# A slot of an attention pipeline put in another order: scores before values, left-over transpositions later

## The chip, the core and the metric

The kernel runs on one core of a Trainium2 chip. The core has a matrix engine (PE; its weight loads are shown apart as PEld), a vector engine (DVE), a scalar engine (ACT), a general engine (POOL) and a queue that issues the DMAs (SP). Each engine takes its instructions strictly in the order in which the kernel emits them, and they wait for each other through semaphores. The metric is the time of one launch on the device in microseconds (us).

## The reference

`x` is [8, 256, 512], eight batch entries. Four layers follow each other, each added to `x`:

```
x = x + L0(x, cond)        # masked self-attention, 8 heads, queries = keys = values
x = x + L1(x, cond)        # modulated RMS-norm, qkv, normalised q and k, attention of 16 heads, o + o @ W_out
x = x + L2(cond, cond, x)  # 256 Runge-Kutta steps, one after the other
x = x + L3(cond, x)        # a GRU cell, 256 steps
```

What matters of the two attentions:

```
L0:  q = x^T Wq^T;  scores = q q^T / sqrt(32), masked;  ctx = softmax(scores) q;  out = ctx Wo^T
L1:  xn = rmsnorm(x) * g * (1 + scale) + shift;  q, k, v = xn W_qkv;  q, k = rmsnorm per head
     o = softmax(q k^T / sqrt(32)) v;  result = o + o W_out
```

## The kernel before

`attention` computes L0 and L1 for all eight entries; `scans` then computes L2 and L3 step by step and is not touched by the change. `scans` starts at about 929 us of the profiled span.

**Slots.** `attention` is a loop over slots `g` from -5 to 79 (line 463), eight slots per batch entry (`U = 8`). L0 of entry `b` has eight units, (half `e` of the heads) x (key block `kc`); unit n is scored in slot 8b+n-4 (`scores0`), weighted in slot 8b+n+1 (`weights0`) and multiplied with the values in slot 8b+n+2 (`values0`). The L1 work of an earlier entry is spread over the same slots. Once all stages run, a round of eight slots repeats; the table names a slot by `g` modulo 8, and lists what it has besides one unit each of scores, values, weights and maxima.

| g mod 8 | further work in the kernel before |
| --- | --- |
| 1 | `weigh0`; transposition of k, part 1; qkv product of q, part 0; first half of x2 (`modulated_out`) |
| 2 | turn of that half (`modulated_turn`); transposition of q, part 0; `masked_out`; qkv of q, part 1; second half of x2 |
| 3 | turn of the second half; transposition of q, part 1; `project` of the entry after next, `normalize`, `maxima1` (needs the transposed q), `rows0` |
| 4 | `project_out`, `modulate`, `project`, `rows1`, `maxima1`, `weights1` |
| 5, 6 | `project_out` and `weigh0` (5 only), qkv of v, `rows1`, `maxima1`, `values1`, `weights1` |
| 7 | qkv of k, part 0; `rows1`, `values1`, `weights1`, `rows0` |
| 0 | transposition of k, part 0; qkv of k, part 1; `values1` |

**The order inside a slot** is written out by hand (lines 464 to 517), and so is the order on every engine's queue. Left-over work of the slot before comes first (`leave`), then values, scores and weights of L0, then the transposition of q or k that the slot before left (`qkv_out`), and then everything else.

**Units of work.** `scores0` (L192): four products of a 32-row block (L198) into four PSUM banks, evicted by four ACT copies (L203) into a tile `sc`. `maxima0` (L206): one DVE maximum over `sc` (L208). `rows0`: transposes the maxima of four units (L216), copies the row out (L218), sends it to DRAM (L221) and back as the broadcast tile `bc` (L222). `weights0` (L224): DVE subtracts `bc` (L226), ACT takes the exponential (L227). `values0` (L229): two sets of four products (L238) into two banks of their own. `weigh0`: two DVE reciprocals and products (L255, L256), then two POOL operations (L257, L258), which make `ctxT`. `masked_out` (L260): output product of L0 (L265), added by DVE (L268). `qkv` (L300): a product (L305); for q and k two ACT readings (L318, L320), a DVE sum (L326), three POOL operations (L328 to L330) in `qkv_norm`, and in a later slot four transpositions (L340) and an ACT copy (L344) in `qkv_out`. `normalize`: ACT squares (L277), two POOL operations, ACT scaling (L282). `modulated_out` (L401): a product (L405) and a DVE addition (L410). `modulated_turn` (L418): four transpositions (L421), an ACT copy (L426) and a DMA (L428).

**Buffers.** All products but those of L238 take their PSUM banks from one pool of six, tag `s` (L57, L60), handed out in turn, so that an allocation waits for the readers of the sixth one before it. The two banks of L238 are freed by `weigh0`. In SBUF there are six `sc` tiles, four `x` tiles (loaded by L74, read last by L410) and two `bc` tiles.

Of the kernel before, what the change touches and what calls it, by code (L numbers as in the profile page):

```python
# [8 lines left out]
F32 = mybir.dt.float32  # L9
# [5 lines left out]
P = 128  # L15
B, T, D = 8, 256, 512
# [8 lines left out]
def attention(ctx, tc, cst, x, cond, wqT, woT, w_emb, b_emb, g_norm, w_qkv, g_q, g_k, w_out, follow):  # L25
# [21 lines left out]
    U = 8  # L47
# [3 lines left out]
    two = ctx.enter_context(tc.tile_pool(name="a_two", bufs=2))  # L51
# [18 lines left out]
    xs, mks = {}, {}  # L70

    def load(b):
        xs[b] = two.tile([P, 2, D], F32, tag="x", name=f"x_{b}", bufs=4)
        nc.sync.dma_start(xs[b], x[b].rearrange("(k p) t -> p k t", p=P))  # L74
        mks[b] = fone.tile([P, D], F32, tag="mk", name=f"mk_{b}", bufs=2)
        nc.sync.dma_start(mks[b], cond[b].partition_broadcast(P))
# [115 lines left out]
    def scores0(b, e, kc):  # L192

        qm = qms[b]
        ss = [bank([P, D], f"s0_{b}_{e}_{kc}_{h}") for h in range(4)]
        for h in range(4):
            r = 32 * h
            nc.tensor.matmul(  # L198
                ss[h], lhsT=qm[r : r + 32, e, kc * P : (kc + 1) * P], rhs=qm[r : r + 32, e, :], start=True, stop=True
            )  # L200
        sc = ftwo.tile([P, 4, D], F32, tag="sc", name=f"sc_{b}_{e}_{kc}", bufs=6)
        for h in range(4):
            nc.scalar.copy(sc[:, h, :], ss[h])  # L203
        scs[b, e, kc] = sc
# [7 lines left out]
    def rows0(b, e):  # L212

        pt = bank([P, NJ, P], f"pm0_{b}_{e}")
        for qc in range(NJ):
            nc.tensor.transpose(pt[:, qc, :], mxp0[e][:, qc, :], ident)  # L216
        mrow = ftwo.tile([P, D], F32, tag="mrow", name=f"mrow0_{b}_{e}", bufs=1)
        nc.scalar.copy(mrow, pt.rearrange("p q n -> p (q n)"))  # L218
        bc = bcs[b, e] = ftwo.tile([P, 4, D], F32, tag="bc", name=f"bc_{b}_{e}")
        row = dram.tile([4, D], F32, tag="row", name=f"row_{b}_{e}", bufs=2)  # L220
        nc.sync.dma_start(row, mrow.rearrange("(h i) n -> h i n", i=32)[:, 0, :])  # L221
        nc.sync.dma_start(bc, row.rearrange("h n -> (h n)").partition_broadcast(P).rearrange("p (h n) -> p h n", h=4))  # L222
# [6 lines left out]
    def values0(b, e, kc):  # L229
        if kc == 0:  # L230
            if e == 0:
                ctxTs[b] = fone.tile([P, 2, D], F32, tag="ctxT", name=f"ctxT_{b}")
            pc0s[b, e] = [ps_c.tile([P, D], F32, tag=f"c{i}", name=f"pc0_{b}_{e}_{i}") for i in range(2)]
        sc = scs.pop((b, e, kc))
        for half in range(2):
            for h in range(4):
                o = e * P + h * DH
                nc.tensor.matmul(  # L238
                    pc0s[b, e][half][32 * h : 32 * h + 32, :],
                    lhsT=qtoks[b][:, kc, o : o + DH] if half == 0 else ones[:, 0:DH],  # L240
                    rhs=sc[:, h, :],
                    start=(kc == 0),
                    stop=(kc == NJ - 1),
                )
# [55 lines left out]
    def qkv(b, part, m):  # L300

        n = f"{b}_{m}_{part}"
        ps = bank([P, D], f"psqkv_{n}")
        for c in range(NJ):
            nc.tensor.matmul(  # L305
                ps,
                lhsT=xnTs[b][:, c, m * P : (m + 1) * P],
                rhs=wqkv_sb[:, c, part * D : (part + 1) * D],
                start=(c == 0),
                stop=(c == NJ - 1),  # L310
            )
        if part == 2:
            if m == 0:
                vts[b] = two.tile([P, 2, D], F32, tag="vt", name=f"vt_{b}", bufs=2)
            nc.scalar.copy(vts[b][:, m, :], ps)
            return None
        sq = line(f"sq_{n}")
        nc.scalar.activation(sq, ps, AF.Square)  # L318
        qr = line(f"qr_{n}")
        nc.scalar.copy(qr, ps)  # L320
        return sq, qr
# [15 lines left out]
    def qkv_out(b, part, m, qr):  # L337
        pt = bank([P, NJ, P], f"ptqk_{b}_{m}_{part}")
        for c in range(NJ):
            nc.tensor.transpose(pt[:, c, :], qr[:, c * P : (c + 1) * P], ident)  # L340
        ts, tag, g = ((qTs, "qT", gqs), (kTs, "kT", gk_sb))[part]
        if m == 0:
            ts[b] = two.tile([P, NJ, 256], F32, tag=tag, name=f"{tag}_{b}", bufs=1)
        nc.scalar.activation(ts[b][:, :, m * P : (m + 1) * P], pt, AF.Copy, scale=g)  # L344
# [56 lines left out]
    def modulated_out(b, m):  # L401
        n = f"{b}_{m}"
        ps = bank([P, D], f"psx2_{n}")
        for c in range(NJ):
            nc.tensor.matmul(  # L405
                ps, lhsT=oTs[b][:, c, m * P : (m + 1) * P], rhs=wout_sb[:, c, :], start=(c == 0), stop=(c == NJ - 1)
            )
        x2 = line(f"x2_{n}")

        nc.vector.tensor_tensor(  # L410
            x2.rearrange("p (m j i) -> p j m i", j=NJ, m=NJ),
            ps.rearrange("p (j m i) -> p j m i", j=NJ, m=NJ),
            xs[b][:, m, :].rearrange("p (j m i) -> p j m i", j=NJ, m=NJ),
            ALU.add,
        )
        return x2
# [18 lines left out]
    for b in range(B):  # L435
        per = 2 if b >= B - 2 else 1
        norms.append(U * b + U + (2 if b == B - 1 else 3))
        start = norms[b] + (2 if b != B - 2 else 3)
        for i, part in enumerate(PARTS):
            parts.setdefault(start + i // per, []).append((b, *part))  # L440
        HEADS.append(start + len(PARTS) // per)
        OUT.append(HEADS[b] + 6)

    def at(g, rel, n=1):

        b, r = divmod(g - rel, U)
        return (b, r) if 0 <= b < B and r < n else None
# [10 lines left out]
    def leave(kind):  # L458
        for key in [k for k in left if k[0] == kind]:
            yield *key[1:], left.pop(key)  # L460

    with tc.manual_schedule():
        for g in range(-5, OUT[-1] + 3):
            for a in leave("qt"):
                project_out(*a)
            if g == OUT[-1] + 2:
                cst["soon"]()
            for a in leave("x2"):
                modulated_turn(*a)
            if g - 1 in norms:  # L470
                modulate(norms.index(g - 1))
            if a := at(g, 2, U):
                values0(a[0], a[1] // 4, a[1] % 4)
            if a := at(g, -4, U):
                scores0(a[0], a[1] // 4, a[1] % 4)
            if a := at(g, 1, U):
                weights0(a[0], a[1] // 4, a[1] % 4)
            if (a := at(g, 2, U)) and a[1] % 4 == 3:
                weigh0(a[0], a[1] // 4)
            for a in leave("qkv"):  # L480
                qkv_out(*a)

            if a := at(g, -5, 2):
                left["qt", a[0], a[1]] = project(*a)
            if a := at(g, U + 2):
                masked_out(a[0])
            if g == 4:
                modulation()
            if g in norms:
                normalize(norms.index(g))  # L490
            made = [(part, qkv(*part)) for part in parts.get(g, ())]
            for b in range(B):
                if g - OUT[b] in (0, 1):
                    left["x2", b, g - OUT[b]] = modulated_out(b, g - OUT[b])

            for part, lines in made:
                if lines:
                    qkv_norm(*part, *lines)
                    left["qkv", *part] = lines[1]
            if a := heads(g, 1):  # L500
                rows1(*a)
            a, a1 = at(g, -4, U), heads(g, 0)
            last = a and a[1] % 4 == 3
            if last:
                maxima0(a[0], a[1] // 4, 3)
            if a1:
                maxima1(*a1)
            if a2 := heads(g, 2):
                values1(*a2)
            if a2 := heads(g, 1):  # L510
                weights1(*a2)
            if a and not last:
                maxima0(a[0], a[1] // 4, a[1] % 4)
            if last:
                rows0(a[0], a[1] // 4)
            if (a2 := at(g, -7)) and a2[0] > 1:
                load(a2[0])
            if g == U * B + 2:
                first.close()
                follow()  # L520
                for (b, m), d in x2d.items():
                    nc.sync.dma_start(
                        cst["x2T"][:, :, b, m * P : (m + 1) * P], d.rearrange("p (j n) -> p j n", j=NJ)
                    )
# [486 lines left out]
```

## Time and profile before

| | |
| --- | --- |
| device time, median of three runs | 3015.35 us (3013.42 to 3015.56) |
| the profiled execution: its time / its span | 3006.1 us / 3004.3 us |
| mean granted clock of PE in it | 0.973 |
| `attention` / `scans` in the span | 0 to about 929 us / 929 to 3004 us |
| PE, busy share of the span | 90% |
| DVE / ACT / POOL, busy share | 71% / 57% / 35% |
| L305 (qkv products), x384 | 177.0 us busy, 607 ns each |
| L226 (subtraction of the maxima), x64 | 150.1 us busy, 2345 ns each |
| L208 (maxima), x64 | 145.7 us busy, 2279 ns each |
| L203 (score evictions), x256 | 131.1 us busy, 604 ns each |
| L227 (exponentials), x64 | 129.5 us busy, 2024 ns each |

A row of groups gives an instruction's line, its count, its busy time and the idle time of its engine just before it, with what ended it. The profiled execution is 9.25 us shorter than the median of the three timed runs; a sum is made against its own 3004.3 us of span.

### The profile page before, as it was taken

How to read it: one execution, taken by the hardware profiler on the slowest of the kernel's cores; microseconds unless marked ns; L12 is line 12 of the kernel's file. 1: busy time of each engine (PE TensorE's matmuls, PEld its weight loads, DVE VectorE, ACT ScalarE, POOL GpSimd, SP SyncE). 2: the span in 40 equal slices, each digit the busy share in tenths (PEclk: the TensorE clock that was granted, in tenths of full speed). 3: DMA queues.
4: the chain of work that ended last, by engine and by line, in shares of the span. 5: the costliest groups of instructions: out<-in, count | busy, mean ns of one | idle time of the engine just before them, and what ended most of it. 6: DMA issues, size and time to landing. Idle time of an engine off the chain costs nothing.

```text
span 3004.3 us, 159873 instructions
## 1 busy us (share of the span) xinstructions
PE 2713.9 (90%) x67258; PEld 1922.1 (64%) x67258; DVE 2129.0 (71%) x8948; ACT 1715.9 (57%) x8427; POOL 1047.1 (35%) x2945
## 2 busy tenths in 40 slices
PE   6679889888998999999999999999999999999997
PEld 2224334433455777777777777777777777777775
DVE  4657667766535777777777777777777777777774
ACT  4456555655335666666666666666666666666652
POOL 0132222222322444444434444444344444443442
PEclk7789999999999999999999999999999999999999
DMA  3010010101050000000000000000000000000000
GB/s 141 25 39 29 32 46 15 47 32 36 22 120 3 5 6 7 6 7 6 6 7 6 6 7 6 7 6 6 7 6 6 7 6 7 7 6 7 6 6 7
DMA packets 27560, 57.60 MB, mean 19 GB/s; under 512 B 2816, under 2 KB 17164, under 8 KB 24788
## 3 DMA queue, kind: packets, MB, share of 16 engines
q1 hardware_dynamic: 26836, 47.36, 5.1%
q8 instruction: 526, 8.62, 1.2%
q14 instruction: 198, 1.62, 0.2%
HBM read 40.15 MB, written 7.21 MB: 16 GB/s over the span
## 4 chain that ended last, share of the span: by engine, by line
PE 55%; DVE 27%; ACT 8%; issue 4%; POOL 4%; ACTq 0%; DMA 0%; POOLq 0%; SPq 0%; DVEq 0%
PE pg L742 19%; PE ic L707 17%; DVE icT L899 5%; DVE qn L900 5%; PE psqkv L305 4%; ACT tT L607 4%; PE pc L238 3%; DVE hqs L860 3%; DVE own L757 3%; DVE sqmm L856 2%; DVE v L759 2%; POOL r L329 2%; PE s L198 2%; PE pc L154 2%; DVE hz L787 2%
## 5 line engine op out<-in xcount | busy, mean ns | idle before, releaser
L707 PE MATMUL ic<-cT_sb,tT 128*8 128x128 f32 x32736 | 1087.5, 273 | 82.4 <-ACT tT L607 44.3
L707 PEld LDWEIGHTS ic<-cT_sb,tT 128*8 128x8 f32 x32736 | 759.1, 89 | 343.1 <-ACT tT L607 272.2
L742 PE MATMUL pg<-whh_sb,hz 128*32 128x128 f32 x24576 | 818.9, 274 | 49.5 <-DVE hz L787 16.2
L607 ACT ACTIVATE tT<-qn 128x16 f32<-128x16 f32 x2046 | 439.9, 216 | 642.4 <-DVE qn L900 563.9
L742 PEld LDWEIGHTS pg<-whh_sb,hz 128*32 128x32 f32 x24576 | 667.8, 110 | 124.0 <-DVE hz L787 123.6
L899 DVE STREAM_TRANSPOSE icT<-ic 128x64 f32<-128x64 f32 x2048 | 503.4, 246 | 68.3 <-PE ic L707 63.4
L900 DVE SCALAR_TENSOR_TENSOR qn<-icT,hqs 128x16 f32<-128x16 f32 x2048 | 350.4, 171 | 70.0
L702 POOL TENSOR_TENSOR W<-W,cx 128x128 f32<-128x128 f32 x765 | 297.3, 389 | 256.4 <-ACT cx L688 256.3
L695 POOL TENSOR_TENSOR W<-cx,us 128x128 f32<-128x128 f32 x255 | 116.9, 458 | 446.5 <-ACT cx L688 446.5
L856 DVE SCALAR_TENSOR_TENSOR sqmm<-sqmm,qn 128x32 f32<-128x32 f32 x768 | 153.5, 200 | 152.4 <-ACT sqmm L845 123.2
L860 DVE TENSOR_TENSOR hqs<-W,sqmm 128x32 f32<-128x32 f32 x1020 | 200.2, 196 | 46.3 <-DVE sqmm L856 1.4
L203 ACT COPY sc<-s 128x512 f32<-128x512 f32 x256 | 131.1, 604 | 139.4 <-PE s L198 139.4
L721 PE MATMUL gi<-wih_sb,x3T 128*32 128x384 f32 (+2 forms) x3072 | 202.4, 379 | 0.5 <-POOL x3T L912 0.5
L688 ACT ACTIVATE cx<-qn 128x32 f32<-128x32 f32 x1280 | 200.8, 213 | 0.1
L305 PE MATMUL psqkv<-wqkv_sb,xnT 128*128 128x512 f32 x384 | 177.0, 607 | 0.0
L688 ACT ACTIVATE cx<-p 128x32 f32<-128x32 f32 x1020 | 149.8, 217 | 32.8 <-DVE p L855 2.0
L208 DVE TENSOR_REDUCE mxp<-sc 128x4 f32<-128x2048 f32 x64 | 145.7, 2279 | 28.1 <-ACT sc L203 28.1
L226 DVE TENSOR_TENSOR sc<-sc,bc 128x2048 f32<-128x2048 f32 x64 | 150.1, 2345 | 4.3 <-DMA bc<-row 4.3
L757 DVE STREAM_TRANSPOSE own<-pg 128x128 f32<-128x128 f32 x256 | 84.9, 332 | 91.8 <-PE pg L742 91.6
L688 ACT ACTIVATE cx<-q 128x32 f32<-128x32 f32 x1020 | 145.6, 213 | 0.0
L227 ACT ACTIVATE sc<-sc,negT 128x2048 f32<-128x2048 f32 x64 | 129.5, 2024 | 22.6 <-DVE sc L226 15.1
L845 ACT ACTIVATE sqmm<-qn 128x32 f32<-128x32 f32 x768 | 140.5, 183 | 0.6
(149 smaller groups left out, 3338.6 us busy)
## 6 DMA issues: line engine op xcount, KB each, us to landing
bc<-row SPq DMA_DIRECT2D x16, 1024.0 KB
x<-in_x SPq DMA_DIRECT2D x8, 512.0 KB
out<-o SPq DMA_DIRECT2D x256, 16.0 KB
wqkv_sb<-in_L_cond_W_qkv SPq DMA_DIRECT2D x1, 3072.0 KB
wih_sb<-in_L_cond_W_ih SPq DMA_DIRECT2D x4, 768.0 KB
whh_sb<-in_L_cond_W_hh SPq DMA_DIRECT2D x4, 768.0 KB
x2d<-x2o SPq DMA_DIRECT2D x11, 256.0 KB
x2T<-x2d SPq DMA_DIRECT2D x11, 256.0 KB
```

The source lines that it names most:

```text
L305: nc.tensor.matmul(ps, lhsT=xnTs[b][:, c, m * P : (m + 1) * P], rhs=wqkv_sb[:, c, part * D : (part + 1) * D], start=(c == 0), stop=(c == N ...
L607: nc.scalar.activation(tT, src[:, half * HM : (half + 1) * HM, :], AF.Tanh)
L688: nc.scalar.activation(c[:, i], x, AF.Copy, scale=f)
L702: nc.gpsimd.tensor_tensor(W[:, i + 1 : 5], W[:, i + 1 : 5], c, ALU.add)
L707: nc.tensor.matmul(ps[32 * j : 32 * j + B, :], lhsT=tT[k // HM][:, k % HM, :], rhs=cT_sb[:, k, j * P : (j + 1) * P], start=(k == 0), stop= ...
L721: nc.tensor.matmul(gi_ps[rows(j), g0:g1, :], lhsT=x3T[c][:, k, :], rhs=wih_sb[:, k, g0:g1, j * P : (j + 1) * P], start=(k == 0), stop=(k = ...
L742: nc.tensor.matmul(pg_ps[rows(j), :], lhsT=hzs[tau % 3][:, k, 32 * g : 32 * g + 32], rhs=whh_sb[:, k, g, j * P : (j + 1) * P], start=((k, ...
L757: nc.vector.transpose(pgt.rearrange("p m n -> p (m n)"), pg_ps)
L856: stt(mm, sq, LIN[s], qs, ALU.subtract, ALU.mult)
L860: nc.vector.tensor_sub(hq, W[:, s], mm)
L899: nc.vector.transpose(icT.rearrange("p m n -> p (m n)"), ic[:, half * 64 : half * 64 + 64])
L900: stt(qn[:, m2, :], icT[:, :, 0:B], IC[s], hq[:, m2, :], ALU.mult, ALU.add)
```

## The change

Five edits. (1) In a slot the scores of L0 come first, then the values, and only then the left-over work of the slot before. (2) `qkv_out`, the transposition of the q or k that the slot before left, moves from behind the weights to behind this slot's own qkv product (and so behind `project`, `masked_out` and `normalize`). (3) The second half of x2 is made two slots after the first instead of one, except for the last two entries; its turn follows one slot later. (4) Seven `sc` tiles instead of six, because a slot's scores are now written before its values free the oldest tile; five `x` tiles instead of four, because an entry's `x` is read one slot longer. (5) One `bc` tile instead of two. The last slot is 79 in both, and the computation is the same.

```diff
-        xs[b] = two.tile([P, 2, D], F32, tag="x", name=f"x_{b}", bufs=4)
+        xs[b] = two.tile([P, 2, D], F32, tag="x", name=f"x_{b}", bufs=5)
...
-        sc = ftwo.tile([P, 4, D], F32, tag="sc", name=f"sc_{b}_{e}_{kc}", bufs=6)
+        sc = ftwo.tile([P, 4, D], F32, tag="sc", name=f"sc_{b}_{e}_{kc}", bufs=7)
...
-        bc = bcs[b, e] = ftwo.tile([P, 4, D], F32, tag="bc", name=f"bc_{b}_{e}")
+        bc = bcs[b, e] = ftwo.tile([P, 4, D], F32, tag="bc", name=f"bc_{b}_{e}", bufs=1)
...
-        OUT.append(HEADS[b] + 6)
+        OUT.append((HEADS[b] + 6, HEADS[b] + (8 if per == 1 else 7)))
...
-        for g in range(-5, OUT[-1] + 3):
+        for g in range(-5, OUT[-1][1] + 2):
+
+            if a := at(g, -4, U):
+                scores0(a[0], a[1] // 4, a[1] % 4)
+            if a := at(g, 2, U):
+                values0(a[0], a[1] // 4, a[1] % 4)
             for a in leave("qt"):
                 project_out(*a)
-            if g == OUT[-1] + 2:
+            if g == OUT[-1][1] + 1:
                 cst["soon"]()
             for a in leave("x2"):
                 modulated_turn(*a)
             if g - 1 in norms:
                 modulate(norms.index(g - 1))
-            if a := at(g, 2, U):
-                values0(a[0], a[1] // 4, a[1] % 4)
-            if a := at(g, -4, U):
-                scores0(a[0], a[1] // 4, a[1] % 4)
             if a := at(g, 1, U):
                 weights0(a[0], a[1] // 4, a[1] % 4)
...
-            for a in leave("qkv"):
-                qkv_out(*a)
...
             made = [(part, qkv(*part)) for part in parts.get(g, ())]
+            for a in leave("qkv"):
+                qkv_out(*a)
             for b in range(B):
-                if g - OUT[b] in (0, 1):
-                    left["x2", b, g - OUT[b]] = modulated_out(b, g - OUT[b])
+                if g in OUT[b]:
+                    m = OUT[b].index(g)
+                    left["x2", b, m] = modulated_out(b, m)
```

## The prediction

> **What bounds it now.** I read the page first, then the time by windows, then PE, ACT and DVE in order of time.
>
> ```profile
> PEclk7789999999999999999999999999999999999999
> PE 55%; DVE 27%; ACT 8%; issue 4%; POOL 4%; ACTq 0%; DMA 0%; POOLq 0%; SPq 0%; DVEq 0%
> L340 PE MATMUL ptqk<-ident,qr 128*128 128x128 f32 x128 | 23.3, 309 | 52.1 <-POOL qr L330 52.1
> L238 PE MATMUL pc<-sc,qtok 128*32 128x512 f32 x512 | 79.4, 697 | 32.1 <-ACT sc L227 32.0
> 243.40:343.86 100.46, 88.70 (x652) 40.78 (x656) 69.07 (x59) 57.24 (x95) 25.38 (x22) 0.98 0.10 35
> 343.86:442.64 98.78, 87.03 (x653) 40.21 (x656) 69.01 (x59) 57.24 (x95) 25.36 (x22) 1.00 0.10 36
> 442.64:541.40 98.76, 87.00 (x652) 40.19 (x656) 68.99 (x59) 57.23 (x95) 25.38 (x22) 1.00 0.10 36
> 541.40:642.89 101.49, 90.21 (x653) 41.55 (x656) 69.00 (x59) 57.23 (x95) 25.38 (x22) 0.97 0.09 35
> 642.89:742.00 99.11, 88.83 (x631) 40.21 (x631) 65.52 (x54) 54.23 (x88) 24.45 (x21) 0.94 0.08 28
> ```
>
> The scans (929 to 3004 us, lines 607 to 900 of the chain) are untouched. Only the first 929 us can change, in three stages: a ramp (slots up to 19, to 243 us), five rounds of eight slots (the windows; columns: length, busy PE, PEld, DVE, ACT, POOL, clock, DMA), and a tail (742 to 929). In a round PE is busy 87.0 of 98.8 us and idle 11.8; no other engine passes 69. So a round ends with PE, and only its idle time can go. In the ramp nothing is full:
>
> ```profile
> 113.48 2.06 PE L198 MATMUL s<-qm 32*128 32x512 f32 x8
> 119.62 1.93 PE L238 MATMUL pc<-sc,qtok 128*32 128x512 f32 x8 [4.08 <-ACT sc L227]
> 115.62 2.05 ACT L203 COPY sc<-s 128x512 f32<-128x512 f32 x4 [5.02 <-PE s L198]
> 117.53 2.03 ACT L227 ACTIVATE sc<-sc,negT 128x2048 f32<-128x2048 f32 x1
> ```
>
> This is a ring. The values wait for the exponential, which stands on ACT's queue behind the evictions of the same slot's scores, and those scores stand on PE's queue behind the values. Values 3.6, scores 2.1, evictions 1.9 and exponential 2.1 follow one another: 9.7 us a slot (values start at 109.91, 119.62, 129.35).
>
> **Edit 1 in the ramp.** With scores first, the evictions run beside the values and the ring is cut. What is late next is DVE: per slot L226 2.20 and L208 2.19 (start to start), every fourth slot `weigh0` 4.25; and `bc`, which arrives some 7.5 us after the last maximum of its four (transposition and row copy 1.2, row DMA 1.75, issue to first use 4.7: 33.57 to 38.28) while DVE has 5 us of other work, so 2 to 2.5 idle per four slots. That is (4 x 4.4 + 4.25 + 2.3)/4 = 6.0 a slot. PE needs 2.9 (5.7 at half clock), ACT 3.9. I walked DVE, ACT and PE through the slots in their new order with these durations, starting at the first `bc`, which DMA brings at 38.28 as before:
> - slots 2 to 4 (42.7 to 80.3): the modulation's 11.3 us of PE stays, the serial parts around it go: 7 saved.
> - slots 5 to 10 (57.6 us): 43, so 14 saved.
> - slots 11 to 16 (57.7): normalisation, then qkv products; DVE-bound, 50, so 8 saved.
> - slots 17 to 19 (47.7): here edit 2 acts. PE waits for POOL 4.09 + 3.78 + 3.78 and then runs slowly (L305 5.54 for 3.60, L265 5.79 for 3.70, L176 3.62 for 1.98: 5.7 more), 17.3 together; less the new waits below and less that DVE's `weigh0` now sets slot 18: 11 saved.
>
> Together 40. Bounds: 25, if only the ring of slots 5 to 10 and half of the POOL waits go; 50, if DVE never waits for `bc`.
>
> **The rounds.** PE's waits in one round (1.34 in slot 4 besides):
>
> ```profile
> 599.76 0.66 PE L340 MATMUL ptqk<-ident,qr 128*128 128x128 f32 x4 [1.58 <-POOL qr L330]
> 608.16 0.63 PE L421 MATMUL ptx<-ident,x 128*128 128x128 f32 x4 [0.88 <-DVE x L410]
> 613.96 1.11 PE L340 MATMUL ptqk<-ident,qr 128*128 128x128 f32 x4 [2.25 <-POOL qr L330]
> 627.34 0.63 PE L421 MATMUL ptx<-ident,x 128*128 128x128 f32 x4 [0.88 <-DVE x L410]
> 633.14 0.66 PE L340 MATMUL ptqk<-ident,qr 128*128 128x128 f32 x4 [2.24 <-POOL qr L330]
> 639.65 0.33 PE L216 MATMUL pm<-ident,mxp 128*128 128x128 f32 x1 [0.95 <-DVE mxp L208]
> 641.30 0.33 PE L293 MATMUL ptx<-ident,xh 128*128 128x128 f32 x1 [0.88 <-ACT xh L282]
> 587.60 0.42 DVE L165 TENSOR_TENSOR oT<-pc,r 128x256 f32<-128x256 f32 x1
> ```
>
> *Goes:* the two turns (0.88 each), since scores and values (1.07 + 1.86) now hide x2's addition; the transpositions in slots 1 and 2 (1.58, 2.25), behind 3.5 to 7 us of products; the row wait 0.95, hidden by the moved x2 product; and 0.88 + 0.28 before `modulate`, hidden by scores and values. In all 7.7.
> *Stays in part:* the transposition of the last q, in slot 3. From L326 to L340 it takes 6.03 us (627.11 to 633.14), and L326 follows its product by 0.85. Before it stand the transposition 0.5, scores, values and `project` 1.83: 5.3. It waits 6.9 - 5.3 = 1.6 instead of 2.24.
> *Comes (a):* q's copy L344 now stands on ACT behind `project` and `normalize`, and `maxima1` waits for it. From the end of the qkv product: 0.85 to L326, 0.6 + 2.2 + 2.2 through L326, L208, L226, exponential 2.0, L182 to L282 4.3 (by the starts), L344 0.7: 12.8. PE is there after 5.3 + 1.6 + 0.5 + 3.45 (the moved x2 product) = 10.8. Wait 2.0.
> *Comes (b):* scores at a slot's head meet banks that the 1.86 us of values used to cover. By the order of the six banks, slots 6 and 7 have the bank of `values1` as their second, free when L165 ends: 564.27 against 563.80 (0.5), 576.07 against 575.61 (0.5); slot 0 has it as its first: 588.0 against 586.5, less the 0.5 already lost (1.0); slots 2, 4 and 5 some 0.15 to 0.25. In all 2.6. A wait here holds the values too, and all of PE behind them. No row shows it; it lies between 0 and 1.86 for each of these slots, and the DVE row above is the nearest.
>
> Net: 7.7 + 0.6 - 2.0 - 2.6 = 3.7 a round, five rounds: 18. DVE's path through slots 0 to 2 (`values1`, L208, L226, `weigh0`, `ctxT`, then L265) becomes as late as PE's there and hides nothing more. Bounds for the rounds: 0 and 30.
>
> **Clock.** The five rounds are 4.7 us longer than five of 98.78, and their clock falls to 0.94: after an idle of 2.25, L265 took 4.73 in one round. [...] The row with a bank wait (L375, 1.34 idle) is followed by full speed in the round from 541.4 and by slow products (L238 1.94 for 1.06) in the next. [...] I keep the rows: no change.
>
> **Edits that cost nothing.** One `bc` tile: its DMA must wait for the subtraction of the next slot (L226), which ends 2.2 us after the maximum in the ramp, before the row has landed at 3; in slot 3 it starts 1.4 later, with 8 us to spare. If that cover were gone it costs at most 2.5 for each of the four tiles in the ramp. Five `x` tiles: the load no longer blocks SP until L410 (628.1 in slot 2); it follows `bc` at once and shares its DMA engines, as at 112.4, where both took 5.7 us: 1 us, twice in the ramp. The mask load then holds SP until `ctxT`; behind it is only the turn's DMA. Seven `sc` tiles remove no wait, they permit edit 1.
>
> **Tail.** Waits for POOL of 1.06, 2.60, 2.15, 0.51 and 3.74, and L405 at 5.59 for 3.60: 12. Two parts a slot keep POOL busy 4.4 us each, so 1.9 and 3.6 remain, and x2's move in slots 66 and 67 uncovers L367 behind `normalize`, 3. Saved 4 (0 to 8).
>
> **Sum.** 40 + 18 + 4 = 62 us off a span of 3004.3: 2942, with 1.8 around it 2944. The timed runs lie 9.25 above the profiled one, so 3015.35 - 62 = **2953**.
>
> **Rivals.**
> 1. *The rounds keep their length*: the bank and q waits are as large as what goes. For it: (a) and (b) are inferred; against: 7.7 us go for certain. Then 40 + 4 = 44: **2971**. 22%.
> 2. *PE stays at half clock through the ramp*: DVE leaves it idle in every fourth slot, and the page's PEclk begins 7, 7, 8. Six qkv products then take 3.5 more, 21: **2974**. Against: in slots 13 to 15 of the trace (165 to 183 us) they ran at 3.7. 10%.
> 3. *Slower: the banks decide.* If the evictions, behind the exponentials on ACT, never free banks in time, each of the 40 slots of the rounds loses the 1.86 of cover beyond what is gained elsewhere: 74 - 62 = +12, **3027**. It decides from 1.55 us a slot (62/40). Against: L203 to L203 ACT has slack, busy 57 of 99. 10%.
> 4. *It does nothing*, because a wait for the same banks orders scores behind values anyway. Then 3015. The two use different banks. 3%.
>
> The forecast itself: 55%, own range 2935 to 2972. The range 2928 to 2990 adds rivals 1 and 2 with the bounds; out are rivals 3 and 4 and some of each edge. About 6 us (0.2%) is what a measurement tells from no change: faster 0.87, same 0.03, slower 0.10.
>
> **What would show it.** Right: in the ramp, values no longer wait for L227, slots of some 6 us, and the values of slot 20, where the first round begins, starting near 203 instead of 243; no POOL wait at L340 in slots 1 and 2; in slot 3, L340 waits about 1.6 and L352 about 2.0 for ACT L344; at slot heads, L198 waits for DVE L165. Wrong: waits at L198 over 1.5 us in most slots, rounds of 98 us or more, or a first round that starts after 225.

## The result, and the profile after

The changed kernel takes 2959.44 us (median of four runs, 2958.41 to 2963.82) against 3014.39 (3001.57 to 3015.56) before: a ratio of 0.983, 95% interval 0.9802 to 0.9858. The forecast of 2953 was 6 us too low. Its stages missed by more: the profiled execution has a span of 2956.6, so 47.7 us of its 62 are gone, and only the ramp gave what was forecast:

| stage | saved, forecast | saved, measured |
| --- | --- | --- |
| ramp (until slot 20's first work: 240.39 before, 199.79 after) | 40 | 40.6 |
| five rounds (slots 20 to 59: 502.3 before, 496.9 after) | 18 | 5.4 |
| tail (until `scans` begins: 186.5 before, 184.6 after) | 4 | 1.9 |

From the page after: the granted clock in tenths, the chain that ended last, and the groups of the ring.

```profile
PEclk7989999999999999999999999999999999999998
...
PE 39%; DVE 24%; ACT 5%; issue 3%; ACTq 0%; POOL 0%; DVEq 0%; POOLq 0%
...
L227 ACT ACTIVATE sc<-sc,negT 128x2048 f32<-128x2048 f32 x64 | 128.6, 2010 | 89.2 <-DVE sc L226 79.2
...
L226 DVE TENSOR_TENSOR sc<-sc,bc 128x2048 f32<-128x2048 f32 x64 | 147.8, 2310 | 11.9 <-DMA bc<-row 11.9
```

The groups by line add the two rows that were shown of before (52.1 and 32.1 us idle there) and a third:

```profile
L238 PE MATMUL pc<-sc,qtok 128*32 128x512 f32 x512 | 82.7, 723 | 28.2 <-ACT sc L227 16.4 <-DVE ctxT L256 11.9
L352 PE MATMUL n<-kT,qT 32*128 32x256 f32 x512 | 41.5, 412 | 9.7 <-ACT qT L344 9.5 <-DVE oT L165 0.2
L340 PE MATMUL ptqk<-ident,qr 128*128 128x128 f32 x128 | 19.9, 282 | 15.7 <-POOL qr L330 15.6
```

PE's waits for POOL fell from 52.1 to 15.6, and those of the values for the exponential from 32.0 to 16.4 (of which 10.98 stand ahead of the very first values; 9.94 before). New are the values' wait for `ctxT` (11.9) and L352's for q's copy (9.5). The exponential now waits for the subtraction (79.2): the ring is cut, and DVE is late in the ramp. PE, ACT and DVE in order of time, slots 8 to 10 of the ramp, show it (the two ACT rows and the DVE row belong to slots 8 and 9):

```profile
91.96 1.14 PE L198 MATMUL s<-qm 32*128 32x512 f32 x8
93.03 1.06 PE L238 MATMUL pc<-sc,qtok 128*32 128x512 f32 x8
...
97.17 1.06 PE L238 MATMUL pc<-sc,qtok 128*32 128x512 f32 x8 [1.15 <-ACT sc L227]
...
106.16 1.94 PE L238 MATMUL pc<-sc,qtok 128*32 128x512 f32 x8 [5.99 <-DVE ctxT L256]
...
95.09 2.04 ACT L227 ACTIVATE sc<-sc,negT 128x2048 f32<-128x2048 f32 x1
...
101.80 2.00 ACT L227 ACTIVATE sc<-sc,negT 128x2048 f32<-128x2048 f32 x1 [2.74 <-DVE sc L226]
...
99.47 2.29 DVE L226 TENSOR_TENSOR sc<-sc,bc 128x2048 f32<-128x2048 f32 x1 [1.92 <-DMA bc<-row]
...
202.77 1.94 PE L238 MATMUL pc<-sc,qtok 128*32 128x512 f32 x8
```

In slot 8 the values follow the scores directly. Later the exponential waits for DVE, and DVE waits 1.92 us for `bc`. The values of slot 10, at 106.16, wait for two reciprocals and products of `weigh0` on DVE. The last line is slot 20's values: 202.77, where 203 was forecast (243.3 before).

The rounds are the other half. Time by windows, from one `masked_out` to the next (columns as before: length, busy PE, PEld, DVE, ACT, POOL, clock, DMA share, GB/s), after:

```profile
376.92:475.89 98.97, 93.68 (x650) 42.66 (x649) 68.46 (x59) 57.73 (x94) 25.36 (x23) 0.97 0.11 36
475.89:574.86 98.97, 93.68 (x650) 42.66 (x649) 68.47 (x59) 57.70 (x94) 25.37 (x23) 0.97 0.11 36
```

and the same part of a round of before at full clock:

```profile
416.90:515.68 98.78, 87.02 (x651) 40.21 (x649) 69.00 (x58) 57.24 (x95) 25.38 (x22) 1.00 0.10 36
```

The same products, so PE's idle time fell from 11.76 to 5.29 us and its busy time rose from 87.02 to 93.68. Nothing was added to PE: the products themselves became slower. PE in order of time, from slot 4 of one round after to slot 3 of the next, says where:

```profile
299.34 2.06 PE L198 MATMUL s<-qm 32*128 32x512 f32 x8
301.33 1.06 PE L238 MATMUL pc<-sc,qtok 128*32 128x512 f32 x8
...
309.30 0.77 PE L375 MATMUL s<-qT,kT 32*128 32x256 f32 x5 [1.14 <-ACT qt L182]
...
311.42 3.13 PE L198 MATMUL s<-qm 32*128 32x512 f32 x7
...
314.48 1.94 PE L238 MATMUL pc<-sc,qtok 128*32 128x512 f32 x8
...
327.47 2.51 PE L198 MATMUL s<-qm 32*128 32x512 f32 x8
...
340.40 2.51 PE L198 MATMUL s<-qm 32*128 32x512 f32 x8
...
354.21 1.14 PE L198 MATMUL s<-qm 32*128 32x512 f32 x8 [1.21 <-DVE oT L165]
...
363.07 1.14 PE L198 MATMUL s<-qm 32*128 32x512 f32 x8
...
390.71 0.66 PE L340 MATMUL ptqk<-ident,qr 128*128 128x128 f32 x4 [1.49 <-POOL qr L330]
...
396.66 0.71 PE L352 MATMUL n<-kT,qT 32*128 32x256 f32 x8 [1.21 <-ACT qT L344]
```

Free scores take 1.14 (slots 1 to 3 and 0). In slots 4, 6 and 7 they take 2.06, 2.51 and 2.51, and that longer time is not listed as idle: the group began, and then a product in its middle waited for a bank (a row counts two records for each of the four products). Only slot 0, where the first product waits, shows idle time (1.21). In slot 5 of this round both scores and values are slow, values 1.94 for 1.06. The clock by windows of 2 us there:

```profile
310.00:312.00 2.00, 2.00 (x35) 1.59 (x28) 2.00 (x3) 0.66 (x2) 0.24 (x1) 1.00 0.00 0
312.00:314.00 2.00, 2.00 (x7) 0.89 (x4) 2.00 (x2) 2.00 (x5) 0.00 (x0) 0.53 0.03 8
314.00:316.00 2.00, 2.00 (x9) 0.40 (x12) 1.06 (x1) 1.35 (x3) 0.00 (x0) 0.50 0.00 0
316.00:318.00 2.00, 2.00 (x12) 0.20 (x4) 0.00 (x0) 0.00 (x0) 0.00 (x0) 0.50 0.00 0
318.00:320.00 2.00, 2.00 (x11) 1.48 (x8) 1.78 (x2) 0.85 (x2) 0.00 (x0) 0.77 0.00 0
```

Some 7 us at half speed (312.10 to 318.93). In the three rounds of 98.97, from 376.92 on, slot 5 is at full speed. There the clock falls twice for 3.4 us, first in slot 6 and then in slot 0, each time at a bank wait of the scores:

```profile
423.17 3.31 PE L198 MATMUL s<-qm 32*128 32x512 f32 x8
451.55 1.65 PE L198 MATMUL s<-qm 32*128 32x512 f32 x8 [1.20 <-DVE oT L165]
...
425.00:427.00 2.00, 2.00 (x10) 0.20 (x8) 2.00 (x2) 2.00 (x5) 0.00 (x0) 0.50 0.03 8
453.00:455.00 2.00, 2.00 (x16) 0.57 (x16) 0.66 (x1) 1.87 (x4) 0.00 (x0) 0.50 0.01 4
```

In one piece or in two, it is 6.8 us at half speed a round, a mean clock of 0.97. This is called the half-speed stretch below.

### The profile page after: what moved, and what is told of

The parts are those of the page before. It is cut to its first block, busy times and chain, and to the rows that moved or that the text cites. A ratio compares the mean times of both kernels' runs of the same rounds, so it can differ in the third digit from the quotient of the medians.

```text
span 2956.6 us, 159809 instructions
## 1 busy us (share of the span) xinstructions
PE 2720.4 (92%) x67258; PEld 1930.5 (65%) x67258; DVE 2124.6 (72%) x8948; ACT 1720.9 (58%) x8427; POOL 1049.1 (35%) x2945
## 4 chain that ended last, share of the span: by engine, by line
PE 39%; DVE 24%; ACT 5%; issue 3%; ACTq 0%; POOL 0%; DVEq 0%; POOLq 0%
PE pg L744 19%; PE ic L709 18%; DVE icT L901 5%; DVE qn L902 5%; ACT tT L609 4%; DVE hqs L862 3%; DVE own L759 3%; DVE sqmm L858 2%; DVE v L761 2%; DVE hz L789 2%; DVE own L778 1%; ACT sqmm L847 1%; DVE own L784 1%; PE psx L405 1%; ACTq L609 0%
## 5 line engine op out<-in xcount | busy, mean ns | idle before, releaser
L227 ACT ACTIVATE sc<-sc,negT 128x2048 f32<-128x2048 f32 x64 | 128.6, 2010 | 89.2 <-DVE sc L226 79.2
L305 PE MATMUL psqkv<-wqkv_sb,xnT 128*128 128x512 f32 x384 | 174.8, 600 | 0.2 <-DVE oT L165 0.2
L226 DVE TENSOR_TENSOR sc<-sc,bc 128x2048 f32<-128x2048 f32 x64 | 147.8, 2310 | 11.9 <-DMA bc<-row 11.9
L203 ACT COPY sc<-s 128x512 f32<-128x512 f32 x256 | 132.1, 617 | 40.6 <-PE s L198 40.4
L208 DVE TENSOR_REDUCE mxp<-sc 128x4 f32<-128x2048 f32 x64 | 145.8, 2279 | 6.7 <-ACT sc L203 6.7
```

The lines of the kernel that those rows point to most:

```text
L305: nc.tensor.matmul(ps, lhsT=xnTs[b][:, c, m * P : (m + 1) * P], rhs=wqkv_sb[:, c, part * D : (part + 1) * D], start=(c == 0), stop=(c == N ...
```

## The experiments

The theory to test was: edit 1 makes the ramp's gain and costs the rounds (bank waits at slot heads, and a half-speed stretch that they or the new waits bring); edit 2 and edit 3 pay for that in the rounds. The rival: the ramp's gain comes from the later transpositions (edit 2), and the heads of the rounds cost nothing much. The kernel before, run beside these, had medians of 3008.96 to 3012.79 us. A round is measured from one `masked_out` to the next.

**Edit 1 alone**, with seven `sc` tiles and one `bc` tile, on the kernel before; and **edit 2 alone** on it.

```diff
+            if a := at(g, -4, U):
+                scores0(a[0], a[1] // 4, a[1] % 4)
+            if a := at(g, 2, U):
+                values0(a[0], a[1] // 4, a[1] % 4)
             for a in leave("qt"):
...
-            if a := at(g, 2, U):
-                values0(a[0], a[1] // 4, a[1] % 4)
-            if a := at(g, -4, U):
-                scores0(a[0], a[1] // 4, a[1] % 4)
```

```diff
-            for a in leave("qkv"):
-                qkv_out(*a)
...
             made = [(part, qkv(*part)) for part in parts.get(g, ())]
+            for a in leave("qkv"):
+                qkv_out(*a)
```

> The kernel before with edit 1 alone (scores, then values at the head of a slot, seven score tiles, one broadcast tile); transpositions and x2 stay where they were. Theory (the ring of the ramp is cut by edit 1; at the slot heads of the rounds the scores wait for banks and PE then falls to half clock, 9 us a round): slot 20 begins near 211 us instead of 240.4, each round takes 104 to 107 us instead of 98.8, and the two cancel: total within 12 us of before. Rival (the ramp's gain is mostly edit 2's): slot 20 begins after 228. Rival 2 (the heads cost nothing; slot 3 eats the rounds' gain): rounds 95 to 97 us, total 2970.

> The kernel before with edit 2 alone (the transposition of q or k behind this slot's own products). Theory: the POOL waits of slots 17 to 19 shrink, slot 20 begins near 230 us; in a round the waits of 1.58 and 2.25 go, that of 2.24 shrinks by half, but maxima1 now waits some 4 us for L344, since no x2 product stands before it in slot 3: rounds 97.5 to 99.5; total 10 to 20 us less. Rival (late transpositions pay in the rounds, and only the heads lost it): rounds 95, total 30 us less.

Edit 1 alone: 3032.17 us in the median of five, but two of these are 2995 and 2997 and three 3032 to 3041; the ratio of 0.9995 (0.994 to 1.0051) says no more than that it is about as before. Its profile, of one of the two short ones (span 2995.6), shows the two halves: slot 18's `masked_out` at 186.41 (216.79 before), and rounds of 105.9 instead of 98.8 to 104.3.

```profile
396.81:502.69 105.88, 94.66 (x649) 43.97 (x649) 68.67 (x58) 57.80 (x95) 25.45 (x22) 0.97 0.10 33
```

Gain and loss nearly cancel. Edit 2 alone: 2991.09, ratio 0.9938 (0.9922 to 0.9955); slot 18's `masked_out` at 206.35, and rounds of 96.2 to 100.6. L340's waits for POOL fall to 2.2 us over the rounds, and the wait of L352 for L344, 4.7 us long, takes their place:

```profile
527.95 1.24 PE L352 MATMUL n<-kT,qT 32*128 32x256 f32 x8 [4.73 <-ACT qT L344]
...
540.44 0.77 PE L375 MATMUL s<-qT,kT 32*128 32x256 f32 x5 [1.35 <-ACT qt L182]
```

So the ramp's 39 at slot 18 are mostly edit 1's (30) with edit 2 adding 9, and in the rounds edit 1 alone costs some 7 us each, while edit 2 alone gains 9.5 us in all (from slot 18 to slot 66 592.0, 601.5 before). The rival falls.

**Edit 3 taken back** (x2's second half one slot later again), everything else as changed.

```diff
-        OUT.append((HEADS[b] + 6, HEADS[b] + (8 if per == 1 else 7)))
+        OUT.append((HEADS[b] + 6, HEADS[b] + 7))
```

> The changed kernel without edit 3: the second half of x2 one slot after the first again. Theory: the x2 product no longer covers the wait of maxima1 for L344 in slot 3 (1.2 grows to about 4.6), while the wait of 1.5 at the last q's transposition goes, since the product now stands before it: rounds 100 to 101.5 us, total 5 to 15 us more than the changed kernel; the tail 2 to 3 us shorter. Rival (where x2 stands makes no difference, PE only moves its wait): within 3 us of the changed kernel.

2973.29 us, ratio 0.9876 (0.9861 to 0.9891): 14 slower than the changed kernel. Rounds of 100.0 to 103.8, and L352's wait is 4.65 a round in place of 1.21: 3.44 more, what the moved product covers. Its tail, from slot 66's `masked_out`, takes 108.7 instead of 112.5: there the move cost 3.8, close to the 3 forecast.

**The heads of the slots**: values first again from slot 20 on, so that the ramp keeps edit 1 and the rounds lose it.

```diff
+            if g < 20:
+                if a := at(g, -4, U):
+                    scores0(a[0], a[1] // 4, a[1] % 4)
+                if a := at(g, 2, U):
+                    values0(a[0], a[1] // 4, a[1] % 4)
+            else:
+                if a := at(g, 2, U):
+                    values0(a[0], a[1] // 4, a[1] % 4)
+                if a := at(g, -4, U):
+                    scores0(a[0], a[1] // 4, a[1] % 4)
```

> The changed kernel with scores ahead of values only in slots below 20; from slot 20 on, values come first again and scores second. Theory (the heads of slots 4, 5, 6, 7 and 0 lose 7.1 us a round to PSUM banks, and 2.2 us more to the half clock that follows in slot 5): slot 20 still begins near 200, rounds 90 to 92 us instead of 98.9, their granted clock 1.00, total 2920 to 2930. Rival (the rounds lost their gain in slot 3, to L340 and L352): rounds stay at 97 to 99, total 2950 to 2960.

2939.16 us, ratio 0.9765 (0.9751 to 0.978), 20 better than the change. Four rounds of 95.64 to 95.66: the heads cost 98.97 - 95.65 = 3.3 us a round. That is less than half of what was expected, and the half-speed stretch stays, 6.8 us in one piece. It now begins at 404.44, in slot 4, behind a wait for ACT:

```profile
371.68:467.33 95.65, 90.61 (x651) 41.67 (x649) 68.47 (x59) 57.26 (x95) 25.40 (x23) 0.96 0.11 37
...
403.26 0.77 PE L375 MATMUL s<-qT,kT 32*128 32x256 f32 x5 [1.34 <-ACT qt L182]
...
406.00:408.00 2.00, 2.00 (x14) 0.40 (x12) 2.00 (x2) 2.00 (x4) 0.00 (x0) 0.50 0.00 0
```

Bank waits at the heads are therefore not needed to bring the stretch about, although it stood at such waits in the changed kernel.

**q's copy ahead of `normalize`** in slots without a qkv product of their own (slot 3), on that kernel; and then **the last maximum of four ahead of x2's product** in the same slot.

```diff
+            if not parts.get(g):
+                for a in leave("qkv"):
+                    qkv_out(*a)
             if g in norms:
                 normalize(norms.index(g))
```

```diff
+            early = (a := at(g, -4, U)) and a[1] % 4 == 3 and not made
+            if early:
+                maxima0(a[0], a[1] // 4, 3)
             for b in range(B):
                 if g in OUT[b]:
...
-            if last:
+            if last and not early:
                 maxima0(a[0], a[1] // 4, 3)
```

> Values first from slot 20 as in e3; besides, in slots without a qkv product of their own (slot 3 of a round) the last q is transposed ahead of normalize, so that its copy L344 no longer stands behind the normalisation on ACT. Theory (step (a) of the prediction: L352 waits for L344 because of normalize): the wait of 1.2 us at L352 goes, rounds 94.4 us instead of 95.65. [...]

> The kernel with values first from slot 20 and q's copy ahead of `normalize` (2932.78 us, rounds of 95.57), with one more step: in a slot without a qkv product (slot 3) the last maximum of four (L208) is issued ahead of x2's product and its DVE addition (L410), which it stood behind. Theory A (PE's waits add up): the wait of L216 for DVE L208, 7.4 us over the five rounds, goes, rounds 95.57 - 1.5 = 94.1, the whole some 7 us shorter, 2926. Theory B (the clock's windows set the length: a round is a whole number of them while the half-speed stretch comes in every round): rounds stay at 95.57, PE's waits go and slow products take their place; or the half-speed stretch goes with this wait and rounds fall to about 92, 2915 to 2920.

The copy alone: 2932.78 us (0.9746; 0.9726 to 0.9765). L352's wait for L344 is gone, and rounds stay at 95.57: L216 now waits 1.5 us for L208, which stands on DVE behind the addition of the moved x2. A wait was moved. (The whole is 6 us shorter than without it. In the profiles that lies in the eight slots from 18 on, 91.2 us for 96.9.) The granted clock changes in steps of 3.41 us in these profiles (half speed from 424.74 to 428.16 in the one after), and 95.57 is 28 of them: rounds of the same length whatever was taken away suggested that a round has to be a whole number of steps. The last maximum settles that: one round of 92.3 at a clock of 0.98 and three of 93.8 to 93.9 (27.5 steps) at 0.96, these 1.7 less, and 2930.17 us (0.974; 0.9724 to 0.9757). The stretch is still there in all four, in the first for 3.4 us, so waits add up and the steps do not hold the length of the round. In that profile the tail gives part of it back: from slot 66's `masked_out` to `scans` it takes 113.6 us at a clock of 0.92, for 109.3 at 0.97 with the copy alone. The medians differ by 2.6.

**The wait in slot 4 taken away.** L375 waits there for L182, which stands on ACT behind the exponential. In slot 4 the exponential goes behind `rows1`, once on the kernel with values first from slot 20, once on the changed kernel itself.

```diff
         nc.vector.tensor_sub(sc, sc, bcs[b, e])
+
+    def exponential0(b, e, kc):
+        sc = scs[b, e, kc]
         nc.scalar.activation(sc, sc, AF.Exp, bias=negT[:, kc, b : b + 1], scale=SC)
...
                 weights0(a[0], a[1] // 4, a[1] % 4)
+                if (g - 4) % U:
+                    exponential0(a[0], a[1] // 4, a[1] % 4)
...
             if a := heads(g, 1):
                 rows1(*a)
+            if (a := at(g, 1, U)) and (g - 4) % U == 0:
+                exponential0(a[0], a[1] // 4, a[1] % 4)
```

> Values first from slot 20 as in e3; besides, in slot 4 of a round the exponential L227 goes behind rows1 on ACT, so that the readings of psq and of the row maxima (L182, L367) free their banks earlier and weights1 need not wait 1.1 us for them. Theory (this wait, after those of slot 3, sets off the half clock of some 7 us in slots 4 and 5): granted clock of a round 1.00 instead of 0.96, rounds 91 us, total 2910 to 2918. [...]

> The changed kernel (scores first everywhere) with the exponential of slot 4 behind rows1, nothing else. Theory: the wait of 1.1 us in slot 4 goes, and with it the half clock of slot 5; the waits for banks at the slot heads stay: rounds 94 to 95 us, clock 1.00, total 2937 to 2942. Rival (the banks at the slot heads alone set off the half clock): clock stays 0.97, rounds 97.8 to 99, total 2953 to 2960.

The first: 2930.21 us (0.9738; 0.9717 to 0.9759), rounds of 94.99, 91.73, 93.34 and 94.98 at clocks of 0.96, 1.00, 0.98 and 0.96. The second: 2946.37 us (0.9791; 0.9773 to 0.9809), 13 less than the change. The wait falls from 1.14 to 0.21, but most of the gain is the clock's: three of the four rounds are at full clock. The windows price the stretch:

```profile
373.91:469.41 95.50, 91.14 (x651) 42.40 (x649) 68.45 (x59) 57.76 (x94) 25.38 (x23) 1.00 0.11 37
469.41:568.18 98.77, 94.41 (x651) 43.07 (x649) 68.45 (x59) 57.86 (x94) 25.37 (x23) 0.97 0.10 36
```

The same program, two rounds: idle 4.36 in both, busy 3.27 more with the stretch. The round that keeps it is only 0.2 shorter than those of the change (98.77 for 98.97). Its stretch begins at 516.92, in slot 6, and not behind the wait that was taken away. And PE and DVE in order of time of the first of them, in two windows that meet at 421, show a bank wait in slot 6 without the clock in it:

```profile
419.97 1.02 PE L198 MATMUL s<-qm 32*128 32x512 f32 x2
421.11 1.37 PE L198 MATMUL s<-qm 32*128 32x512 f32 x6
...
420.54 0.42 DVE L165 TENSOR_TENSOR oT<-pc,r 128x256 f32<-128x256 f32 x1
```

Two records, those of the first product, then the bank that `values1` holds until L165 ends at 420.96, then six more: 2.51 in place of 1.14, 1.37 lost.

**Idle time filled.** Does PE's idling in slot 3 bring the stretch on? Useless products, overwritten by the real ones, fill it: `project` computed twice (1.8 us), and in a second kernel a quarter of x2's product (0.9) as well.

```diff
-        for k in range(2):
+        for k in (0, 1, 0, 1) if e == 0 and b > 2 else (0, 1):
```

```diff
+        if m == 1 and b < B - 2:
+            nc.tensor.matmul(ps, lhsT=oTs[b][:, 0, m * P : (m + 1) * P], rhs=wout_sb[:, 0, :], start=True, stop=True)
```

> The changed kernel; in slot 3, for the entries from the fourth on, the product of `project` (L176) is computed twice into the same bank, the second overwriting the first: 1.8 us of useless work for PE where it now waits 1.49 at L340 for POOL. By the waits alone the round keeps its 98.97: L340 starts 0.34 later, and L352 waits 0.87 instead of 1.21, since its releaser L344 is bound by `normalize` (L282). Theory A (the half-speed stretch of slot 5 is the answer to PE's short idles in slots 3 and 4, as taking away one of them in slot 4 suggested): the stretch goes in most rounds, the clock is 1.00 there, rounds of 95.7, the whole 2945 to 2950 against 2959.4. Theory B (the stretch is not caused by this idle): 98.9 to 99.3 a round in all, clock 0.97, 2959 to 2962.

> As the last one, and a quarter of the product of x2's second half (L405, 0.9 us) computed once more ahead of it in slot 3, which overwrites it: PE works through what is left of the wait at L352 too, so that slot 3 holds no idle at all; left are the 1.14 at L375 in slot 4 and the 1.2 at the head of slot 0. By the waits alone the round is 0.03 longer. Theory A: clock 1.00 in nearly all rounds, 95.7 a round, 2943 to 2947. Theory B: 99.0 a round, clock 0.97, 2959 to 2962.

2957.38 us (0.9816; 0.9793 to 0.9839) and 2955.33 us (0.9811; 0.9792 to 0.9831): as the change. With the first filler the rounds are 100.27, 98.71, 98.98 and 98.97, and the wait at L340 is gone from them. With both they are 99.26, 96.56, 101.13 and 99.25, one at full clock. New in the second is a wait of L216 for L208 of 0.79 a round, which I had not foreseen, so slot 3 was not free of idle time. The theory that slot 3's idle time brings the stretch on is not borne out. Taking away the wait in slot 4 freed three rounds of four on the changed kernel, but only one, and half of another, with values first from slot 20.

**All together.** Values first from slot 20, q's copy early, the exponential late in slot 4, and x2's second half moved but for the last three entries; then the last maximum too.

```diff
-        OUT.append((HEADS[b] + 6, HEADS[b] + (8 if per == 1 else 7)))
+        OUT.append((HEADS[b] + 6, HEADS[b] + (8 if b < B - 3 else 7)))
```

> The additions of e4 and e6 together, and the second half of x2 of entry 5 back to the next slot, as in the kernel before. Theory: no half clock, waits of 1.2 and 1.1 gone, rounds 89.5 to 90.5 us; slot 66 no longer uncovers the row copy behind normalize, tail 3 us shorter; total 2900 to 2910. Rival (half clock stays): rounds 92 to 95.6, total 2920 to 2935.

> The fastest kernel so far (exponential late in slot 4, second half of x2 moved but for the last three entries, 2921.16 us) with the last maximum of four ahead of x2's product in slot 3. Theory A: 1.5 us a round less, 2914. Theory B: no change in rounds that hold a half-speed stretch (95.0), 1.5 us or more less in those that do not (91.7 to 90.2); between 2914 and 2921, according to how many rounds keep the stretch.

2921.16 us (0.9713; 0.969 to 0.9735) and **2912.75 us** (0.9682; 0.9667 to 0.9696), the best of all, 47 below the change. Of the last one's rounds three of four are at full clock (one of four without the last maximum's move):

```profile
358.77:448.77 90.00, 87.52 (x650) 41.14 (x649) 68.44 (x59) 57.11 (x95) 25.37 (x23) 1.00 0.11 39
448.77:542.04 93.27, 90.79 (x650) 42.27 (x649) 68.55 (x59) 57.12 (x95) 25.38 (x23) 0.96 0.11 38
```

Busy PE of 87.52 is nearly the 87.02 of before, and 2.48 of idle time are left of 11.76. The stretch costs 3.27 here too.

## Why the prediction was right, and where not

**The total** came closer than its parts, and that is luck. In the profiles 14.3 of the forecast 62 us are missing. The sum took the timed runs to lie 9.25 above the profiled one; the changed kernel's median lies only 1.03 above its own, and that made up for 8.2 of the 14.3.

**The ramp** came out by its own parts. By the values' starts, slots 2 to 4 gave 8.4 with what came before (forecast 7), slots 5 to 10 took 43.0 (43), slots 11 to 16 took 52.3 (50), slots 17 to 19 took 35.5 instead of 47.7 (12 saved, 11 forecast). The wait for `bc` is 1.92 where 2 to 2.5 was put. Edit 1 alone, which took 30 us from the ramp while it slowed the rounds, shows that the ring was the main cause in the ramp.

**The rounds: what goes** went. L340's waits in slots 1 and 2, the turns' and the wait before `modulate` are gone; L340 keeps 1.49 in slot 3 (1.6). The row wait was larger than the 0.95 shown, 1.43 in the round from 416.90, and went too.

**Comes (a)**, `maxima1` behind q's copy: 1.21 for 2.0. The mechanism was right, as the kernel with q's copy early shows, and the size a little too large.

**Comes (b)**, bank waits at the heads, 2.6 forecast: too small. Undone in the rounds it gives 3.3. By its own rows it is 0.92, 1.37 and 1.37 in slots 4, 6 and 7 (over 1.14) and 1.21 in slot 0, 4.9 without slot 5. Slots 6 and 7 were put at 0.5 each. The bank is later than that, 0.92 by the idle time of PE's weight loads in the first row below, and the rest of the 1.37, some 0.45, is that the six records left take 1.37 where six of eight in a row take about 0.93 (an estimate between 0.71 for four and 1.14 for eight). Slots 4 and 5 were put at 0.15 to 0.25 by the order of the banks; in the trace the weight loads wait there for DVE L360 (`maxima1`, slot 4) and ACT L390 (slot 5):

```profile
424.28 0.63 PEld L198 LDWEIGHTS s<-qm 32*128 32x128 f32 x6 [0.92 <-PE s L198]
399.05 0.30 PEld L198 LDWEIGHTS s<-qm 32*128 32x128 f32 x4 [0.31 <-DVE mxp L360]
410.75 0.29 PEld L198 LDWEIGHTS s<-qm 32*128 32x128 f32 x2 [0.38 <-ACT ex L390]
```

The undoing gives back 1.6 less than the rows. Of this 1.2 are waits that values first has of its own: 0.77 for `ctxT` at the values of slot 2, 0.22 for L296 and 0.20 more at L375.

**Clock**, "I keep the rows: no change": this is the step that failed. The stretch costs 3.27 a round, as two rounds of one kernel show in two kernels, and 6.8 us of it come in every one of the four rounds that the profile after has from slot 26 on. The rows that I kept were the wait of 1.34 in slot 4, which full clock followed in one round of before and half clock in the next; they do not say what new waits bring. Waits at PSUM banks stand right at the stretch in three of these rounds (inside the scores of slot 6, which take 3.31 there, and 1.20 ahead of those of slot 0). But they are not needed: with the heads covered the stretch stays, behind a wait for ACT of 1.34.

The sum of the rounds, redone as an estimate: at full clock the changed round would be 98.97 - 3.27 = 95.7, which is 3.1 below 98.78, near the 3.7 forecast, because (a) and the row wait paid for (b). Five rounds: 15.5. The clock takes 5 x 3.27 = 16.4 where the 4.7 of the rounds before had been left in: 11.7 more. That leaves 3.8; measured are 5.4. So **rival 1, that the rounds keep their length, came true**, and with it the sign of being wrong that was named, rounds of 98 us or more. The clock did it more than the banks and q waits that the rival named. Rivals 2 to 4 did not come true.

**Tail**: two waits for POOL remain, 1.73 and 3.44 (1.9 and 3.6), and x2's move costs 3.8 (3). Saved 1.9 for 4, within the 0 to 8. **Edits that cost nothing**: one `bc` tile against two was not tried. DVE's whole wait for `bc` grew from 4.3 to 11.9 us, near the 2 to 2.5 per four slots of the ramp that the sum held for the row's way.

**What brings the stretch** was not settled by an edit, but the fourteen traces hold a measure that sorts it. In them the granted clock is 1.00 or 0.50 and changes only at multiples of 3.41 us (in the profile after at 312.10, 318.93, 424.74, 428.16, 452.05 and so on). Take each such step at full clock between 200 and 740 us, count a product record as 0.43 us for 512 columns (eight of L305 take 3.60, four 1.88), and weigh it by the size that its row names: 128\*128, the largest in the rows, counts whole, 32\*128 and 128\*32 a quarter. Where these sums filled less than 0.35 of the step, the clock was halved next, in 92 steps of 92; above 0.40 in 1 of 1857; between in 15 of 81. Idle time alone does not sort them: of 204 steps with 1 us of it or more, 75 were followed by half clock. In the rounds after from 376.92 on, the wait of 1.20 ahead of slot 0's scores fell into the steps from 448.64, 547.62 and 646.61, which came to 0.31 to 0.33, and half clock followed each. In the round of before from 416.90 the wait of 1.34 in slot 4 fell into two steps, which came to 0.61 and 0.42, and full clock followed both. The fillers worked in slot 3, where the steps came to about 0.5 already. **Still open** is whether this is the cause: no run changed it and nothing else.

## What to carry to other kernels

Where an order written out by hand serves a stage in which nothing is full and one in which an engine is, look for a ring through two in-order queues in the first, and cut it there only: scores first alone saved 30 us of the ramp, and it cost 3.3 us a round where PE was full. Compare busy time, not only idle time, before and after: a wait inside a group of products (scores of 2.51 for 1.14) and a lowered clock (values of 1.94 for 1.06) both showed as busy here. And when a removed wait gives nothing, look what stands at the next one: q's copy and the maximum had to go together to shorten the rounds.

## What was not expected of the hardware

Some 7 us at a granted clock of 0.50, in one piece or two, came back in every one of the four rounds of 99 us that the profile after has from slot 26 on, though PE is idle nowhere in the round longer than 1.5 us at a time. They cost 3.27 us, by two rounds of one kernel with 4.36 us of idle time each. Idle time alone did not sort the steps of 3.41 us (half clock followed 75 of the 204 with 1 us of it or more); the count by the products' sizes did, as all 92 filled to less than 0.35 were followed by half clock. Taking away one wait of 1.14 freed three rounds of four in one kernel and one in another; putting products into waits of the slot before freed none or one. The eight records of a slot's scores take 1.14 us in a row; with a bank wait after the second, the remaining six alone take 1.37.
